# A hybrid attention and FFN kernel: the FFN's inner grid values turned in bf16 with their scales spread apart by DMA, and attention B's features normalized ahead

## The chip, the cores and the metric

The kernel runs on one core of a Trainium2 chip. The metric is the device time of one execution in microseconds (us). A core has five engines that run side by side, each with its own queue in order: TensorE (PE in the profile, with its weight loads as PEld), VectorE (DVE), ScalarE (ACT), GpSimd (POOL) and SyncE (SP), which here only issues DMAs.

## The reference

The input x is 4 x 2048 tokens of width 256, all in float32. Four residual layers follow each other; each adds to x a function of the layer-normalized x:

- attention A: three projections, a random-feature map of the whole-tensor-normalized q and k, and `out = s * v / s`, so that the output is the value projection times a ratio near one.
- FFN, used twice with the same weights. Its linear layers work on values quantized in blocks of 16 and turned back: `q = GRID[searchsorted(MID, |x/scale|)] * sign(x) * scale`, with `scale = max|x| / 6` of the block. The gate and up projections go to 704 columns, `h = silu(gate) * up` is quantized in its turn (44 blocks of 16 in a row), and the down projection brings it back to 256.
- attention B, between the two FFNs: q, k, v and two gates are projected; q and k are normalized in each head of 16; the four rows of the batch are mixed for each token (`A = k v^T` summed over the batch, then `q A`), gated, and projected by Wo.

## The kernel before, in words

The 2048 positions are cut into 16 groups of 128. A group holds a tile x of 128 partitions by 4 batch rows by 256, and goes through attention A, FFN, attention B and FFN; a batch row of it in an FFN is called a tile here, so there are 16 x 2 x 4 = 128 FFN tiles. All matmuls take float32 operands.

A first pass loads all of x, sums its Gram matrix for the whole-tensor norm of attention A (L551), and folds and centers the weights: `center` (L903 on) takes the column means out of a weight matrix, so that a projection of x itself is a projection of x minus its mean.

The order of the work is not that of the code. Every operation is recorded with an engine, an assumed duration, a rank and the buffers that it reads and writes; `Plan.order` (from L114) plays these through with its assumed durations and writes out one order for each engine. Ranks are the group's entry in the table BEGIN plus an offset, with a little noise from a seed. Operations marked `port=True` are kept from running on DVE and POOL at the same time. Buffers come from small pools, and an operation is only placed where a buffer of its pool is free. The chip then runs each engine's list strictly in order, with semaphores between the engines; a list does not adapt when a duration was assumed wrongly.

An FFN tile (`ffn_tile`) goes like this:

1. PE: two halves of 352 columns, each with a gate bank and an up bank, 4 recorded matmul calls for a half (L1363).
2. ACT: silu of the gate bank (L1384). DVE: times the up bank into h (L1395).
3. `quantize`: DVE takes the block maxima and their reciprocals (L384, L385); ACT divides the maxima by 6 (L1192); DVE scales h (L389); ACT makes magnitudes in bf16 (L395); DVE rounds to the grid by adding and subtracting a large number (L402, L405); POOL multiplies by the scales (L1220), 704 columns in float32.
4. PE turns the six blocks of 128 columns (L1418, matmuls against an identity; the last two blocks overlap, since 704 is not a multiple of 128), into two banks of 4 and 2 blocks; ACT copies each to SBUF as hqT (L1430).
5. PE: six matmul calls of 256 columns against wdT (L1441). DVE adds the result to x (L339 in the first FFN, L1473 in the second, after which SP stores the row, L1481).

`ffn_in` normalizes x (ACT, L378), quantizes it in the same manner on 128 x 1024 tiles, POOL included, and turns it (L1122, L1129).

`attention_b` turns x as it is (L1122, PE, and L1129, ACT), projects it (L1145) to a bank of 512 columns (q and k) and one of 288 (v and gates), and DVE drains each bank with one operation, `bank * rstd + bias` (L1528). `root` makes rstd of the variances on POOL in 8 small steps, 6 for attention B, which needs no offset.

The profile counts each float32 matmul call against weights twice (x2048 for 1024 calls in L1363) and each float32 turn once.

Of the kernel before, what the change touches and what calls it, by code (L numbers as in the profile page):

```python
# [18 lines left out]
P = 128  # L19
# [230 lines left out]
def kernel(  # L250
# [56 lines left out]
    def load_x(dst, j):  # L307
# [10 lines left out]
    bqkB = one([P, 2 * D], "bqkB")  # L318
    bvgB = one([P, NV], "bvgB")
# [4 lines left out]
    norm_tiles = {k: one([P, NJ, 6, S], f"norms_{k}") for k in ("a", "f1", "b", "f2")}  # L324


    moments = one([P, NJ, S, 6], "moments")
    both = one([P, NJ, S, 2], "both")
    norms = {
        (k, j): [t[:, j, n, :] for n in range(6)]  # L330
# [26 lines left out]
    def take_rstd(key, step):  # L357
# [5 lines left out]
        elif step == 2:  # L363
            nc.gpsimd.tensor_mul(t, y, y)
        elif step == 3:
            nc.gpsimd.tensor_mul(t, t, v)
        elif step == 4:
            nc.gpsimd.tensor_scalar(t, t, -0.5, 1.5, ALU.mult, ALU.add)
        elif step == 5:
            nc.gpsimd.tensor_mul(y, y, t)  # L370
        elif step == 6:
            nc.gpsimd.tensor_mul(off, sums, y)
        else:
            nc.gpsimd.tensor_scalar(off, off, -1.0 / D, 0.0, ALU.mult, ALU.add)
# [29 lines left out]
    def from_sum(a, m):  # L404
        nc.vector.scalar_tensor_tensor(a, m, FLOOR, a, ALU.max, ALU.subtract)  # L405
# [18 lines left out]
    tiles("sx", 3, [P, 3, S * D // BLK], fp)  # L424
    tiles("sil", 2, [P, HF], fp)
    tiles("qa", 4, [P, FF], fp)
    tiles("qm", 2, [P, FF], fp, BF16)
    tiles("sh", 5, [P, 3, FB], fp)
    tiles("hqT", 2, [P, 6, P], fp)
    tiles("tok", 1, [P, S, D], fp)  # L430
    tiles("vz", 2, [P, S, 2 * D], bp)
# [12 lines left out]
    def first_pass():  # L444
# [5 lines left out]
        for b in XN:  # L450
            nc.gpsimd.memset(b.ap[:, :, D : D + 1], 1.0)
        WQK, PROD, WNAT = (plan.given("pp", 0) for _ in range(3))
# [4 lines left out]
        wnat = WNAT.ap.rearrange("p (t c) d -> p t c d", t=2)  # L457
        MK, GROW, MAPT, G = (plan.given(p, 0) for p in ("vz", "tok", "sc", "fac"))
# [32 lines left out]
        for at, token, fn in (  # L491
# [23 lines left out]
            (34.1, ("bB", 0), over_rows(bqkB[:, :D], b_bq)),  # L515
            (34.2, ("bB", 0), over_rows(bqkB[:, D:], b_bk)),
            (34.3, ("bB", 0), over_rows(bvgB[:, :D], b_bv)),
            (34.4, ("bB", 0), over_rows(bvgB[:, D : D + NH], b_br)),
            (34.5, ("bB", 0), over_rows(bvgB[:, D + NH :], b_bw)),
# [105 lines left out]
        for ns in together:  # L625
            for n in ns:
# [21 lines left out]
                for s in range(S):  # L648
# [8 lines left out]
                        [("moments", j, s)],  # L657
# [5 lines left out]
            seen = [("moments", i, s) for i in js for s in range(S)]  # L663
# [239 lines left out]
        def center(at, w, n, tokens):  # L903
# [10 lines left out]
            def dve():  # L914
                for c in range(KC):
                    nc.vector.scalar_tensor_tensor(
                        w[:, c, :], mm.ap[:, :n], -1.0 / D, w[:, c, :], ALU.mult, ALU.add
# [3 lines left out]
            op("DVE", 0.2 + n / 450.0, at + 2, dve, [(mm, 0)], tokens)  # L921
# [16 lines left out]
        center(AHEAD + 50.0, wqkB, 2 * D, [("wqkB", 0)])  # L938
        center(AHEAD + 54.0, wvgB, NV, [("wvgB", 0)])
# [139 lines left out]
        (-91, -18, -64, 57, -73, -13),  # L1079
        (35, 82, 59, 126, 299, 228),  # L1080
        (293, 397, 356, 450, 375, 486),
        (370, 404, 412, 488, 580, 596),
        (433, 471, 475, 573, 630, 638),
        (485, 530, 525, 621, 687, 715),
        (518, 567, 530, 673, 716, 745),
        (588, 644, 630, 743, 560, 676),
        (602, 669, 606, 752, 637, 771),
        (671, 699, 702, 801, 719, 886),
        (714, 797, 826, 891, 958, 1069),
        (788, 865, 877, 996, 972, 1083),  # L1090
        (839, 971, 923, 1030, 822, 1063),
        (879, 1027, 930, 1059, 1017, 1130),
        (910, 1041, 830, 1087, 873, 1230),
        (953, 1023, 1012, 1151, 918, 976),
    ]

    def group(j):
# [65 lines left out]
        def root(at, key):  # L1163

            n = 6 if key[0] == "b" else 8
# [11 lines left out]
        def quantize(at, src, parts, a, m, q, us):  # L1177

            v = blocks_of(src)
            op(  # L1180
# [6 lines left out]
            )  # L1187
            op(
                "ACT",
                0.25,  # L1190
                at + 2,
                lambda: nc.scalar.mul(q.ap[:, 1, :], q.ap[:, 0, :], 1.0 / 6.0),  # L1192
                [(q, 0)],
                [(q, 1)],
# [10 lines left out]
            op("ACT", us["abs"], at + 2, lambda: to_steps(m.ap, a.ap), [(a, 0)], [(m, 0)])  # L1205
            for i, step in enumerate((to_sum, from_sum)):
                op(
                    "DVE",
                    us["pass"],
                    at + 4 + 0.1 * i,  # L1210
                    lambda step=step: step(a.ap, m.ap),
                    [(m, 0)],
                    [(a, 0)],
                    port=True,
                )
            op(
                "POOL",
                us["scale"],
                at + 6,
# [6 lines left out]
            )  # L1226

# [96 lines left out]
        def ffn_in(at, k):  # L1324
# [4 lines left out]
            for s in range(S):  # L1329
# [10 lines left out]
            quantize(  # L1340
# [6 lines left out]
                {"amax": 1.8, "pass": 1.19, "abs": 1.0, "scale": 1.93},  # L1347
            )
            return turn(
# [4 lines left out]
        def ffn_tile(at, k, s, xqT):  # L1354
            h, qa, qm, sh = (plan.buf(p) for p in ("h", "qa", "qm", "sh"))
            for half in range(2):
# [46 lines left out]
            quantize(  # L1403
# [6 lines left out]
                {"amax": 1.32, "pass": 0.86, "abs": 0.74, "scale": 1.4},  # L1410
            )
            hqT = plan.buf("hqT")
            for i0, i1 in ((0, 4), (4, 6)):
# [360 lines left out]
```

## Time and profile before

| | us |
|---|---|
| median of 3 runs | 1522.6 (1521.85 to 1522.8) |
| the profiled execution | 1523.6 |
| its span, first to last instruction | 1521.6 |
| PE busy | 1499.4 (99%) |
| PE weight loads busy | 1073.0 (71%) |
| DVE busy | 1387.3 (91%) |
| ACT busy | 810.1 (53%) |
| POOL busy | 693.2 (46%) |

The mean granted TensorE clock is 0.997 of full speed. In a row of groups, "x2048 | 637.7, 459 | 0.3" reads: 2048 instructions, together busy for 637.7 us, 459 ns from start to end of one on average, and 0.3 us of idle time before them. Matmuls overlap each other, so the mean of one times their number is more than their busy time; the spacing of a matmul's starts, which is what the next one has to wait, is read from a timeline. In a timeline, a line gives start, length, engine, line of the code, operation and the number of equal instructions merged into it.

### The profile page before, as it was taken

What the parts mean: (1) busy time and instruction counts of PE and PEld (TensorE: products, weight loads), DVE (VectorE), ACT (ScalarE), POOL (GpSimd) and SP (SyncE); (2) the same over time, 40 slices, a digit from 0 to 9 for tenths busy, and PEclk for the clock granted to TensorE, in tenths of its full rate; (3) what the DMA queues carried; (4) which work ended last, traced back from release to release, by engine and by line L of the source; (5) the groups of instructions that cost most, each with busy time, mean ns of one, the idle gap of its engine ahead of it and who ended that gap; (6) DMA issues with size and microseconds to landing.
All of it is one profiled execution on the core that took longest, in us unless ns stands there. A gap on an engine that the chain in (4) does not pass through costs nothing.

```text
span 1521.6 us, 18780 instructions
## 1 busy us (share of the span) xinstructions
PE 1499.4 (99%) x6362; PEld 1073.0 (71%) x6362; DVE 1387.3 (91%) x2266; ACT 810.1 (53%) x1745; POOL 693.2 (46%) x750
## 2 busy tenths in 40 slices
PE   7989999999999999999999999999999999999999
PEld 6847676766767666677667676776677677667777
DVE  6899999899899998989999999898989899999985
ACT  6666455555636556455554455465654455445443
POOL 5444454444536254444543543544453644553531
PEclk9999999999999999999999999999999999999999
DMA  8300000000000000000000000100000000000000
GB/s 268 100 1 1 1 1 0 29 0 11 18 4 7 18 4 5 8 4 22 4 18 8 8 21 14 42 5 4 5 7 1 0 1 1 5 11 14 14 22 21
DMA packets 29025, 27.68 MB, mean 18 GB/s; under 512 B 3585, under 2 KB 28673, under 8 KB 28929
## 3 DMA queue, kind: packets, MB, share of 16 engines
q1 hardware_dynamic: 28928, 26.49, 5.6%
q8 instruction: 50, 0.82, 0.2%
q14 instruction: 47, 0.38, 0.1%
HBM read 18.09 MB, written 8.39 MB: 17 GB/s over the span
## 4 chain that ended last, share of the span: by engine, by line
PE 80%; DVE 15%; issue 2%; ACT 1%; DMA 1%; POOL 0%; SPq 0%; DVEq 0%; POOLq 0%; ACTq 0%
PE bank L1363 32%; PE bank L1441 19%; PE bank L1145 18%; PE bank L1418 5%; PE bank L1122 3%; PE bank L551 2%; DVE h L1395 1%; DVE sh L384 1%; DVE pp L1546 1%; DVE qa L402 1%; DVE sc L1553 1%; DVE qa L389 1%; DVE qa L405 1%; DVE fac L1586 1%; DVE qk L1528 1%
## 5 line engine op out<-in xcount | busy, mean ns | idle before, releaser
L1363 PE MATMUL bank<-wguT,turned 128*128 128x352 f32 x2048 | 637.7, 459 | 0.3 <-DVE h L1395 0.3
L1363 PEld LDWEIGHTS bank<-wguT,turned 128*128 128x128 f32 x2048 | 379.7, 190 | 193.8 <-issue 11.7
L1220 POOL TENSOR_TENSOR qa<-qa,sh 128x704 f32<-128x704 f32 x128 | 203.0, 1586 | 407.6 <-DVE qa L405 315.6
L1441 PE MATMUL bank<-wdT,hqT 128*128 128x256 f32 x1536 | 350.6, 380 | 0.4 <-DVE x L1473 0.4
L1441 PEld LDWEIGHTS bank<-wdT,hqT 128*128 128x128 f32 x1536 | 289.5, 190 | 55.6 <-issue 4.5
L1430 ACT COPY hqT<-bank 128x512 f32<-128x512 f32 (+1 forms) x256 | 114.5, 479 | 94.6 <-PE bank L1418 92.4
L1384 ACT ACTIVATE sil<-bank 128x352 f32<-128x352 f32 x256 | 116.1, 458 | 88.9 <-PE bank L1363 83.5
L395 ACT ACTIVATE qm<-qa 128x704 bf16<-128x704 f32 (+1 forms) x136 | 105.9, 781 | 106.4 <-DVE qa L389 103.4
L1395 DVE TENSOR_TENSOR h<-sil,bank 128x352 f32<-128x352 f32 x256 | 128.8, 508 | 19.1 <-PE bank L1363 11.3
L1654 POOL TENSOR_TENSOR pp<-vg,sc 128x1024 f32<-128x1024 f32 x64 | 131.0, 2066 | 31.8 <-DVE tok L1675 27.1
L402 DVE SCALAR_TENSOR_TENSOR qa<-qm,qa 128x704 f32<-128x704 bf16 (+1 forms) x136 | 125.5, 924 | 12.0 <-ACT qm L395 11.9
L389 DVE SCALAR_TENSOR_TENSOR qa<-sh,h 128x704 f32<-128x704 f32 x128 | 126.7, 994 | 2.2
L1145 PE MATMUL bank<-wvz,turned 128*128 128x512 f32 x256 | 119.4, 604 | 5.5 <-ACT turned L1129 4.0
L405 DVE SCALAR_TENSOR_TENSOR qa<-qm,qa 128x704 f32<-128x704 bf16 (+1 forms) x136 | 122.1, 898 | 3.0
L384 DVE TENSOR_REDUCE sh<-h 128x44 f32<-128x748 f32 x128 | 119.1, 931 | 3.7
L1145 PE MATMUL bank<-wqkB,turned 128*128 128x512 f32 x256 | 119.6, 593 | 0.0
L1129 ACT COPY turned<-bank 128x512 f32<-128x512 f32 x160 | 86.8, 588 | 58.3 <-PE bank L1122 58.1
L1418 PEld LDWEIGHTS bank<-ident,qa 128*128 128x128 f32 x768 | 90.7, 141 | 29.0 <-issue 12.0
L1220 POOL TENSOR_TENSOR qax<-qax,sx 128x1024 f32<-128x1024 f32 x32 | 68.3, 2135 | 87.2 <-DVE qax L405 81.8
L1418 PE MATMUL bank<-ident,qa 128*128 128x128 f32 x768 | 105.0, 273 | 1.2 <-POOL qa L1220 1.1
L1192 ACT ACTIVATE sh<-sh 128x44 f32<-128x44 f32 x128 | 30.6, 239 | 119.2 <-DVE sh L384 116.3
L1145 PEld LDWEIGHTS bank<-wvz,turned 128*128 128x128 f32 x256 | 47.2, 193 | 54.3 <-issue 41.5
(180 smaller groups left out, 2150.1 us busy)
## 6 DMA issues: line engine op xcount, KB each, us to landing
x<-in_L_attn_a_x_dram SPq DMA_DIRECT2D x23, 512.0 KB, 5.5
out_dram<-x SPq DMA_DIRECT2D x64, 128.0 KB, 1.7
hqT<-in_L_ffn_w_down_dram SPq DMA_DIRECT2D x2, 352.0 KB, 3.9
hqT<-in_L_ffn_w_gate_dram SPq DMA_DIRECT2D x5, 128.0 KB, 3.9
hqT<-in_L_ffn_w_up_dram SPq DMA_DIRECT2D x5, 128.0 KB, 2.7
x<-in_L_attn_a_x_dram SPq DMA_DIRECT2D x4, 128.0 KB, 2.3
pp<-in_L_attn_a_Wq_dram SPq DMA_DIRECT2D x2, 256.0 KB, 5.6
pp<-in_L_attn_a_Wk_dram SPq DMA_DIRECT2D x2, 256.0 KB, 5.2
```

Source lines behind the costliest of these rows:

```text
L384: nc.vector.tensor_reduce(amax, src, AX.X, ALU.max, apply_absolute_value=True)
L389: nc.vector.scalar_tensor_tensor(blocks(a), over_blocks(rs), -6.0 * BELOW, src, ALU.mult, ALU.mult)
L402: nc.vector.scalar_tensor_tensor(a, m, FLOOR, a, ALU.max, ALU.add)
L405: nc.vector.scalar_tensor_tensor(a, m, FLOOR, a, ALU.max, ALU.subtract)
L1145: nc.tensor.matmul(bank.ap[:, :n], lhs.ap[:, c, s * P : (s + 1) * P], w[:, c, :], start=(c == 0), stop=(c == KC - 1),)
L1220: lambda: nc.gpsimd.tensor_mul(blocks(a.ap), blocks(a.ap), over_blocks(q.ap[:, 1, :])),
L1363: nc.tensor.matmul(bank.ap[:, :HF], xqT.ap[:, c, s * P : (s + 1) * P], w[:, c, cols], start=(c == 0), stop=(c == KC - 1),)
L1384: lambda g=g, sil=sil: nc.scalar.activation(sil.ap, g.ap[:, :HF], AF.Silu),
L1395: lambda u=u, sil=sil, half=half: nc.vector.tensor_mul(h.ap[:, half * FB // 2 : (half + 1) * FB // 2, :BLK], blocks(sil.ap), blocks(u.ap[: ...
L1418: nc.tensor.transpose(bank.ap[:, (i - i0) * P : (i - i0 + 1) * P], qa.ap[:, HC[i] : HC[i] + P], ident,)
L1441: nc.tensor.matmul(o.ap[:, :D], hqT.ap[:, i, :], wdT[:, i, :], start=(i == 0), stop=(i == 5),)
L1654: nc.gpsimd.tensor_mul(pv.ap.rearrange("p t (n e) -> p t n e", e=HD), vg.ap[:, :, :D].rearrange("p t (n e) -> p t n e", e=HD), over_blocks ...
```

## The change

The FFN's inner quantization (step 3 and 4 above) is split. `quantize` becomes `to_grid`, which ends with the rounded grid values, without scales. These are small multiples of one half and are written as bf16 into qm. Now there are two paths for a tile:

- values: PE turns six blocks in bf16 (L1494 in the new file), all into one bank; ACT copies the 768 columns, as bf16, into qm (L1505).
- scales: PE turns the 44 block maxima (L1279, float32, 44 x 128 out), ACT divides them by 6 into sT (L1287), and SP issues six DMAs (L1296), each of which reads 8 rows of sT 16 times and writes a 128 x 128 part of hqT.

POOL multiplies hqT by the turned values in place (L1513, 768 columns, one operand float32 and one bf16), and the down matmuls (L1524) follow. The outer quantization in `ffn_in` keeps its POOL product (`times_scales`).

In attention B, ACT normalizes x into a new tile xh (rstd and offset, as in the FFN), xh is turned in place of x, and the two banks are drained by plain copies on ACT (L1619). The biases are folded into the weights: `center` subtracts (mean - bias/256) per row of the weights, and `root` takes 8 steps and ends with an offset raised by one for attention B, so that every feature carries an added 1 which brings in the bias.

Pools: sx 3 to 2, qa 4 to 3, qm 2 to 4 (768 columns), sh 5 to 4, hqT 2 to 3, and new sT (2) and xh (1). Statistics of the first pass and the biases move into tiles that are unused then; norm tiles are shared by two groups. The table BEGIN has new values throughout and the seed of the order goes from 2 to 10, so nearly all of the order of the work is new.

The core of the diff:

```diff
@@ to_grid (was quantize)
-        def quantize(at, src, parts, a, m, q, us):
+        def to_grid(at, src, parts, a, m, q, us, to=None):
...
-            op(
-                "ACT",
-                0.25,
-                at + 2,
-                lambda: nc.scalar.mul(q.ap[:, 1, :], q.ap[:, 0, :], 1.0 / 6.0),
-                [(q, 0)],
-                [(q, 1)],
-            )
...
+            op(
+                "DVE",
+                us["pass"],
+                at + 4.1,
+                lambda: from_sum(a.ap, m.ap[:, :n], to and to.ap[:, :n]),
+                [(a, 0), (m, 0)],
+                [(to or a, 0)],
+                port=True,
+            )
@@ new
+        def scales_turned(at, q, dst):
+            bank, sT = plan.buf("bank"), plan.buf("sT")
+            op("PE", 0.12, at,
+                lambda: nc.tensor.transpose(bank.ap[:FB, :P], q.ap[:, 0, :], ident),
+                [(q, 0)], [(bank, 0)])
+            op("ACT", 0.22, at + 0.5,
+                lambda: nc.scalar.mul(sT.ap, bank.ap[:FB, :P], 1.0 / 6.0),
+                [(bank, 0)], [(sT, 0)])
+            def spread():
+                n = P // BLK
+                for i, f in enumerate(HC):
+                    src = sT.ap[f // BLK : f // BLK + n]
+                    nc.sync.dma_start(
+                        dst.ap[:, i, :], src.unsqueeze(1).to_broadcast([n, BLK, P])
+                    )
+            op("SP", 4.9, at + 1, spread, [(sT, 0)], [(dst, "scale")], land=3.3)
@@ ffn_tile
             hqT = plan.buf("hqT")
-            for i0, i1 in ((0, 4), (4, 6)):
...
+            scales_turned(at + 8, sh, hqT)
+            bank = plan.buf("bank")
+            def turn_hidden():
+                for i, f in enumerate(HC):
+                    nc.tensor.transpose(
+                        bank.ap.bitcast(BF16)[:, i * P : (i + 1) * P],
+                        qm.ap[:, f : f + P],
+                        ident16,
+                    )
+            op("PE", 0.36, at + 14, turn_hidden, [(qm, 0)], [(bank, 0)])
+            op("ACT", 0.73, at + 15,
+                lambda: nc.scalar.copy(qm.ap, bank.ap.bitcast(BF16)[:, : 6 * P]),
+                [(bank, 0)], [(qm, 0)])
+            op("POOL", 1.6, at + 16,
+                lambda: nc.gpsimd.tensor_mul(
+                    hqT.ap, hqT.ap, qm.ap.rearrange("p (c n) -> p c n", n=P)
+                ),
+                [(qm, 0), (hqT, "scale")], [(hqT, 0)], port=True)
@@ attention_b
-            xT = turn(at, X, range(S), lambda: X.ap)
+            xh = plan.buf("xh")
+            for s in range(S):
+                op("ACT", 0.52, at + 1.0 + 0.1 * s,
+                    lambda s=s: normalize(xh.ap[:, s, :], xs(s), key, s),
+                    [(X, s), (key, "rstd")], [(xh, s)])
+            xT = turn(at + 1.5, xh, range(S), lambda: xh.ap)
...
-                        "DVE",
+                        "ACT",
                         ds,
                         at + 5 + 3 * s,
-                        lambda bank=bank, n=n, bvec=bvec, dst=dst, s=s, rstd=rstd: (
...
+                        lambda bank=bank, n=n, dst=dst, s=s: nc.scalar.copy(
+                            dst.ap[:, s, :], bank.ap[:, :n]
                         ),
@@ center
+                if bias:
+                    less, part = bias[0], 1.0 / D
+                    nc.vector.scalar_tensor_tensor(
+                        less, mm.ap[:, :n], -1.0, less, ALU.mult, ALU.add
+                    )
@@ end
-    order = plan.order(2)
+    order = plan.order(10)
```

## The prediction

> **What bounds the kernel now.** First the page's busy times, the chain of work that ended last, and PE's own waits (engine, line, whom it waited for: us in total, times, longest).
>
> ```profile
> PE 1499.4 (99%) x6362; PEld 1073.0 (71%) x6362; DVE 1387.3 (91%) x2266; ACT 810.1 (53%) x1745; POOL 693.2 (46%) x750
> ```
> ```profile
> PE 80%; DVE 15%; issue 2%; ACT 1%; DMA 1%; POOL 0%; SPq 0%; DVEq 0%; POOLq 0%; ACTq 0%
> ```
> ```profile
> PE bank L551 <- ACT vg L378: 10.0, 1, 10.0
> PE bank L1145 <- ACT turned L1129: 4.0, 1, 4.0
> PE bank L1418 <- POOL qa L1220: 1.1, 2, 0.6
> ```
>
> PE never waits long after its start. A busy PE can still be a slack one, so I take issue spacings from a timeline with full queues:
>
> ```profile
> 904.26 2.53 PE L1363 MATMUL bank<-wguT,turned 128*128 128x352 f32 x8
> ...
> 906.63 0.82 PE L1418 MATMUL bank<-ident,qa 128*128 128x128 f32 x6
> ...
> 907.28 5.35 PE L1441 MATMUL bank<-wdT,hqT 128*128 128x256 f32 x24
> ...
> 912.47 4.90 PE L1363 MATMUL bank<-wguT,turned 128*128 128x352 f32 x16
> ```
>
> Starts: 2.37 us for 8, so 296 ns at 352 columns; 0.65 for 6, so 108 ns for a turn; 5.19 for 24, so 216 ns at 256. All are 0.84 ns a column. Times the counts: L1363 606, L1441 332, L1145 337 (512 at 512 columns, 256 at 288, 256 at 256), 1408 turns 152, the first pass about 54: together **1481 us of issue in a span of 1521.6**. The other 41 are 10.0 at the start, 4.0 once, some 3 after the last matmul, and 24 in small gaps. PE is the bound; DVE at 91% is next.
>
> **The change, part by part.** The rows that it touches, the first four from the groups kept apart by shape:
>
> ```profile
> L1430 ACT COPY hqT<-bank 128x512 f32<-128x512 f32 x128 | 74.5, 585 | 51.6 <-PE bank L1418 49.8
> L1430 ACT COPY hqT<-bank 128x256 f32<-128x256 f32 x128 | 47.7, 373 | 43.0 <-PE bank L1418 42.6
> L1528 DVE SCALAR_TENSOR_TENSOR qk<-bank,norms_b,bqkB 128x512 f32<-128x512 f32 x64 | 46.8, 737 | 13.9 <-PE bank L1145 13.6
> L1528 DVE SCALAR_TENSOR_TENSOR vg<-bank,norms_b,bvgB 128x288 f32<-128x288 f32 x64 | 32.1, 503 | 3.6 <-PE bank L1145 1.8 <-POOL norms_f L372 1.0 <-POOL norms_b L370 0.2
> ```
> ```profile
> L1220 POOL TENSOR_TENSOR qa<-qa,sh 128x704 f32<-128x704 f32 x128 | 203.0, 1586 | 407.6 <-DVE qa L405 315.6
> L1418 PE MATMUL bank<-ident,qa 128*128 128x128 f32 x768 | 105.0, 273 | 1.2 <-POOL qa L1220 1.1
> ```
>
> *PE, on the path.* 768 float32 turns become bf16, and 128 float32 turns of scales (128 columns, 108 ns: 13.8 us) are new. No bf16 matmul is in the trace. A turn of float32 weights and data costs 108 ns; bounds for bf16 are no gain (108) and half for half the bytes (54). I take 54: turns and products of float32 cost the same 0.84 ns a column, so the price goes with what is streamed, and bf16 streams half of it (an inference, not a row). -768 x 0.054 + 13.8 = **-27.6 us**; at 108 it is +13.8.
>
> The Trainium skill, "TensorE: Matmul & The Clock Gate", section "Back-to-back issue gap", speaks against it: a steady stream of weight loads and 128-column matmuls runs at about 81 ns each. By that estimate the turns save 20.7 and the part is worth -6.9, which the losses below eat up: no change. No row here has such a pair in bf16.
>
> *DVE, beside PE.* 128 drains leave (46.8 + 32.1 = 78.9 us); the first pass gains two small operations. 1387 - 79 = 1308 over some 1500, 87%. L405 now writes bf16; its row stays at 0.91. Nothing is late next here: between any two FFN tiles of the new order DVE's work falls ever further behind PE's.
>
> *ACT, beside PE.* Out: L1430, 122.2 us. In: 128 copies of 768 columns at (585-373)/256 = 0.83 ns a column, so 797 ns, 102 us; 64 drains at 0.585 and 64 at 0.40, 63; 64 normalizations at 0.593, 38. The scaling of 128 tiny tiles stays at 0.24. 810 + 81 = 891, 60%.
>
> *POOL, beside PE.* 768 columns for 704 (undisturbed 1.39 us): 1.52, or 1586 x 768/704 = 1730 with waits, +18 us; 32 more root steps of 0.32, +10. 48%. If a bf16 operand were slower I bound it by another 0.5, 64 us of an engine that is half idle.
>
> *Normalizing ahead.* Attention B's turn now waits for eight POOL steps (909.48 to 913.90 in the timeline, 4.4 us) and four normalizations (2.4 us). Other groups' FFN tiles lie beside it; without them it would be 16 x 6.8 us.
>
> *SP and the spread.* 768 new DMAs. Issue time from SP's timeline, landing time and packets from the page:
>
> ```profile
> 35.10 0.54 SPq L479 DMA_DIRECT2D pp<-in_L_attn_a_Wk_dram  x1
> 35.69 0.48 SPq L479 DMA_DIRECT2D wqkB<-in_L_attn_b_Wk_w_dram  x1
> ```
> ```profile
> q1 hardware_dynamic: 28928, 26.49, 5.6%
> hqT<-in_L_ffn_w_up_dram SPq DMA_DIRECT2D x5, 128.0 KB, 2.7
> ```
>
> Six issues take 3.0 us, the last lands 2.7 later: 5.7; SP is busy for 384 us. Queued behind are 64 stores and 8 loads of x, needed late. 5.6% of 16 x 1521.6 us over 28928 packets is 47 ns a packet; 768 packets a tile over 16 engines are 2.3 us. No row has SBUF as the source: I bound the spread by 2.7 (one landing alone) and 11 us (twice the estimate), and take 5.7, whose issue part is measured.
>
> The skill, "DMA: Bandwidth & Descriptors", section "Why a DMA increments its semaphore by 16 and not by 1", says that the slowest dimensions, here 8 rows and 128, set the engines: 8 of 16. By that estimate a DMA moves for 0.75 us, longer than an issue, the spread takes some 7 us and is still hidden.
>
> *New waits, read from the built order of the changed kernel* with PE's spacings summed between two of its instructions:
> - From the end of a down product to the next one on the same hqT (SP waits for it, then POOL): at least 10.6 us of PE work, save three at the very end with 5.2, 6.3 and 6.3. Needed: 5.7 + 1.52 + semaphores, about 8. Hidden but for the tail.
> - From a tile's last hidden matmul to the turn of its scales, which holds up all of PE's list: 11 tiles under 3.0 us. Needed: 0.46 + 0.51 + 0.93 + 0.43 and semaphores, about 3. At 3.0 the shortfalls sum to 3 us, at 3.5 to 9; I take 5.
> - From the value turns to the down product: 10 tiles under 3.0, needed 0.80 + 1.52 + semaphores; shortfalls 2 to 4, I take 1, as the rest shares stalls with the former.
>
> *The tail.* Before:
>
> ```profile
> 1508.14 0.89 DVE L405 SCALAR_TENSOR_TENSOR qa<-qm,qa 128x704 f32<-128x704 bf16 x1
> ...
> 1509.20 1.39 POOL L1220 TENSOR_TENSOR qa<-qa,sh 128x704 f32<-128x704 f32 x1 [6.22 <-PE bank L1441]
> ...
> 1513.05 5.45 PE L1441 MATMUL bank<-wdT,hqT 128*128 128x256 f32 x24
> ```
>
> PE works until 1518.5. In the new order the last tile's hqT is freed only by the down product four places from the end, which itself stands behind the last turns: spread, POOL and product follow one another (5.7 + 1.5 + 2.6) where three others of 2.6 cover 5.2. **+4 us.**
>
> **The sum.** 1521.6 - 27.6 + 5 + 1 + 4 = 1504 of span. Part of the 24 us of gaps should go with DVE's relief, for which I take 2 off: 1502. The profiled execution took 1523.6, 2.0 more than its span, and the median of the runs, 1522.6, is 1.0 below that; so the same 1.0 goes on top of the span: **1503**.
>
> **Rivals.**
> - *DVE was half the bound.* The chain gives it 15%. If ten more of the 24 us go: 1490. For it: DVE at 97% from 1200 to 1400. Against: PE's listed waits on DVE are under 2 us.
> - *The turns gain little* (65 to 85 ns): 1511 to 1527. For it: weight loads appear in their own instructions in the new order. Against: loads in the turns of before (141 ns each) hide entirely.
> - *It doesn't do what it says:* a bf16 turn costs 108 ns, 1503 + 41.5 = 1544, slower.
> - *The spread becomes PE's wait.* One mechanism: SP may refill an hqT only after its down product, and PE's next one on it waits for the landing and POOL. Shortfalls in the order: 16 us in all if the way takes 11, 23 at 12, 44 at 14. The tail's 4 stand for the 6 that the order has at 8. The gain of some 20 is gone where the sum is 26, near 12.3, that is, at a spread of 10 instead of 5.7; at 14 the time is about 1503 + 44 - 6 = 1541. For it: no SBUF source, no repeated row in the trace. Against: SP's issues, and 10.6 us of cover.
>
> **Chances.** Forecast .56 (own range 1495 to 1511); DVE's relief .10; little gain .14 (.09 faster, .05 within); 108 ns .08; the spread .12. A measurement of this kernel tells 0.2% from no change. Faster .75, within 0.2% .05, slower .20. The range reaches from 1487 (relief) to 1528 (turns at 85, or a spread of 10 with the forecast's turns); the two slow cases past it are the .20 left out. The unknown prices run on to 1544.
>
> **What would show it.** Turns: starts of the bf16 matmuls 54 ns apart, the six done in 0.33 us. Path: PE still at 98% or more, its issue sum 1453. Spread: hqT landing within 6 us of the first issue, POOL's product waiting for ACT's copy and not for a DMA. Scales: PE's waits on L385 in single microseconds. DVE near 87%. Wrong if PE's idle time grows by over 20 us, or if turns cost over 80 ns.

## The result and the profile after

The changed kernel takes 1546.35 us (median of 6 runs, 1544.01 to 1549.92), the kernel before 1521.78 (1521.25 to 1522.8): a ratio of 1.0163 (1.0150 to 1.0177). It is slower by 25 us, where 20 us less were predicted. The profiled execution has a span of 1542.0 us and a time of 1544.01.

From the page of the changed kernel, the busy times and the chain of work that ended last:

```profile
PE 1488.9 (97%) x6490; PEld 1045.9 (68%) x6490; DVE 1390.9 (90%) x2140; ACT 880.4 (57%) x1808; POOL 749.7 (49%) x782
...
PE 70%; DVE 16%; issue 4%; POOL 4%; ACT 3%; DMA 2%; SPq 0%; POOLq 0%; ACTq 0%; DVEq 0%
```

PE has less work in a longer span. DVE lost 126 instructions, 78.9 us of them drains, and is busier than before (1387.3). PE's own waits (engine, line, whom it waited for: us in total, times, longest) were 10.0, 4.0 and then single us before; now a row of others stands behind the first:

```profile
PE bank L567 <- ACT vg L378: 8.9, 1, 8.9
PE bank L1524 <- POOL hqT L1513: 8.0, 8, 2.5
PE bank L567 <- ACT qk L378: 7.4, 3, 4.0
PE bank L1494 <- DVE qm L405: 5.6, 4, 2.1
```

The wanted part of the change is there. A timeline of the changed kernel (start, length, engine, line):

```profile
906.33 0.50 PE L1494 MATMUL bank<-ident,qm 128*128 128x128 bf16 x6
...
906.66 0.71 PE L1147 MATMUL bank<-ident,xh 128*128 128x128 f32 x5
```

Six bf16 turns start within 0.33 us, 55 ns each.

**A ledger of PE.** Busy time counts pipelined matmuls too long, so I part PE's time otherwise: for each matmul, the spacing of its start from the start before, less the median spacing of that earlier matmul's line (a line with several weight tiles is kept apart by them). The medians sum to the work, the rest is waiting. The columns count time from the first matmul's start, some 9 us into the span. From the traces, us:

| kernel | work | waiting | of it in 0 to 200 | 200 to 1400 | 1400 on |
|---|---|---|---|---|---|
| before | 1499.0 | 9.1 | -0.5 | 9.3 | 0.3 |
| after | 1472.6 | 57.0 | 15.3 | 26.4 | 15.4 |

In every kernel the first pass's Gram matmuls of 257 and of 129 columns share one median, so some 13 us of waiting in the first 200 us are counted as work. Kept apart by shape, the work is 1485.8 us before and 1459.2 after, near the 1481 and 1453 of the prediction, and the waiting 22.4 and 70.4. The differences are the same either way, and they count. The work fell by **26.4 us** (predicted: 27.6). The waiting grew by **48**, and in three places: at the start, throughout, and in the last 140 us. The experiments go by these three.

### The profile page after: what moved, and what is told of

It reads as the page before. It is cut to its first block, busy times and chain, and to the rows that moved or that the text cites. A ratio compares the mean times of both kernels' runs of the same rounds, so it can differ in the third digit from the quotient of the medians.

```text
span 1542.0 us, 21280 instructions
## 1 busy us (share of the span) xinstructions
PE 1488.9 (97%) x6490; PEld 1045.9 (68%) x6490; DVE 1390.9 (90%) x2140; ACT 880.4 (57%) x1808; POOL 749.7 (49%) x782
## 4 chain that ended last, share of the span: by engine, by line
PE 70%; DVE 16%; issue 4%; POOL 4%; ACT 3%; DMA 2%; SPq 0%; POOLq 0%; ACTq 0%; DVEq 0%
PE bank L1438 31%; PE bank L1524 16%; PE bank L1170 15%; PE bank L1147 3%; PE bank L1494 2%; DMA hqT<-sT 2%; DVE qa L402 2%; DVE qa L389 1%; DVE pp L1631 1%; DVE sh L384 1%; POOL hqT L1513 1%; DVE h L1470 1%; PE bank L567 1%; DVE qm L405 1%; DVE sc L1638 1%
## 5 line engine op out<-in xcount | busy, mean ns | idle before, releaser
L1513 POOL TENSOR_TENSOR hqT<-hqT,qm 128x768 f32<-128x768 f32 x128 | 232.0, 1818 | 367.7 <-ACT qm L1505 203.2
L1524 PE MATMUL bank<-wdT,hqT 128*128 128x256 f32 x1536 | 353.1, 382 | 9.7 <-POOL hqT L1513 8.0
L1524 PEld LDWEIGHTS bank<-wdT,hqT 128*128 128x128 f32 x1536 | 290.2, 191 | 70.0 <-POOL hqT L1513 17.8
L402 DVE SCALAR_TENSOR_TENSOR qa<-qm,qa 128x704 f32<-128x704 bf16 (+2 forms) x136 | 141.2, 1038 | 13.8 <-ACT qm L395 13.6
L1739 POOL TENSOR_TENSOR pp<-vg,sc 128x1024 f32<-128x1024 f32 x64 | 132.9, 2093 | 22.4 <-DVE tok L1760 19.3
L389 DVE SCALAR_TENSOR_TENSOR qa<-sh,h 128x704 f32<-128x704 f32 x128 | 139.4, 1098 | 0.8
L1505 ACT COPY qm<-bank 128x768 bf16<-128x768 bf16 x128 | 101.0, 795 | 60.3 <-PE bank L1494 58.5
L405 DVE SCALAR_TENSOR_TENSOR qm<-qm,qa 128x704 bf16<-128x704 bf16 x128 | 126.8, 993 | 4.6 <-POOL norms_f L363 0.5
L1263 POOL TENSOR_TENSOR qax<-qax,sx 128x1024 f32<-128x1024 f32 x32 | 74.0, 2314 | 102.0 <-DVE qax L405 69.9
L384 DVE TENSOR_REDUCE sh<-h 128x44 f32<-128x748 f32 x128 | 119.2, 931 | 4.1
L1631 DVE TENSOR_TENSOR pp<-qk 128x1024 f32<-128x1024 f32 x64 | 83.9, 1310 | 7.8 <-ACT qk L1619 7.6
L378 ACT ACTIVATE xn<-x,norms_f 128x256 f32<-128x256 f32 x128 | 67.8, 594 | 19.4 <-POOL norms_f L372 16.2
L1638 DVE TENSOR_REDUCE sc<-pp 128x64 f32<-128x1024 f32 x64 | 77.6, 1212 | 1.4
```

The source lines that it names most:

```text
L384: nc.vector.tensor_reduce(amax, src, AX.X, ALU.max, apply_absolute_value=True)
L389: nc.vector.scalar_tensor_tensor(blocks(a), over_blocks(rs), -6.0 * BELOW, src, ALU.mult, ALU.mult)
L405: nc.vector.scalar_tensor_tensor(a if to is None else to, m, FLOOR, a, ALU.max, ALU.subtract)
L1513: lambda: nc.gpsimd.tensor_mul(hqT.ap, hqT.ap, qm.ap.rearrange("p (c n) -> p c n", n=P)),
L1524: nc.tensor.matmul(o.ap[:, :D], hqT.ap[:, i, :], wdT[:, i, :], start=(i == 0), stop=(i == 5),)
L1739: nc.gpsimd.tensor_mul(pv.ap.rearrange("p t (n e) -> p t n e", e=HD), vg.ap[:, :, :D].rearrange("p t (n e) -> p t n e", e=HD), over_blocks ...
```

## The experiments

All times are medians; "before" was run beside each and stayed at 1521.6 to 1521.9. Where a kernel's order is called unchanged, only what an operation issues was edited, so that the lists of all engines stand as in the changed kernel.

### First four: spread, product, VectorE, seed

**e1, no spread.**

```diff
             def spread():
                 n = P // BLK
+                return
...
-                    hqT.ap, hqT.ap, qm.ap.rearrange("p (c n) -> p c n", n=P)
+                    hqT.ap, ones.unsqueeze(1).to_broadcast([P, 6, P]),
+                    qm.ap.rearrange("p (c n) -> p c n", n=P),
```

> The order of the changed kernel, unchanged, but the 768 DMAs that spread the scales are left out and POOL's product multiplies by ones (scales left out of the down product). Theory A, the spread is what comes late (27 of POOL's products wait for a landing, 120 us of POOL's idle time): without it the time is 1503 to 1512. Theory B, the port: POOL's product, no longer released by VectorE's rounding, runs beside VectorE's port operations and both get longer (VectorE 1391 us busy where 1308 was forecast): VectorE stays above 1370 and the time stays at 1535 to 1546. Theory C, the order itself is a worse one on the chip: 1535 to 1546 too.

Measured: 1537.7 us, DVE 1385.6. The spread costs 8.6 us and is not the main cause; theory A as put falls.

**e2, thin product.**

```diff
-                    hqT.ap, hqT.ap, qm.ap.rearrange("p (c n) -> p c n", n=P)
+                    hqT.ap[:, 0, :], hqT.ap[:, 0, :], qm.ap[:, :P]
```

> The order of the changed kernel, unchanged, with its DMAs, but POOL multiplies only 128 of the 768 columns (the other five blocks keep the scales alone as hqT), about 0.3 us instead of 1.64. Theory A (the spread is late): POOL still waits for the landings; only the product's own 1.3 us goes from the way, so 1525 to 1540. Theory B (the port): VectorE's rounding operations go back to 0.88 to 0.92 us each, VectorE falls to 1310 to 1330 us, and the time to 1500 to 1512. Theory C (the order): 1535 or more.

Measured: 1519.8 us, DVE 1322.7. DVE goes where theory B put it, the time does not quite, though it is nearest to B; and the edit also shortens each tile's way (from its turns to its down product) by 1.3 us; e5 and e18 part the two.

**e3, attention B's drains back on VectorE.**

```diff
-                        lambda bank=bank, n=n, dst=dst, s=s: nc.scalar.copy(
+                        lambda bank=bank, n=n, dst=dst, s=s: nc.vector.tensor_copy(
                             dst.ap[:, s, :], bank.ap[:, :n]
```

> The order of the changed kernel, but attention B's 128 drains are plain copies on VectorE again instead of ScalarE: 79 us more for VectorE (1391 to 1470), 63 less for ScalarE. Nothing of the computation changes. Theory A (the spread is late, VectorE has slack): within 10 us of the changed kernel, 1540 to 1556. Theory B (VectorE, lengthened at the port, is what PE waits for in small pieces): half of it or more shows, 1575 to 1625. Theory C says nothing of it.

Measured: 1585.2 us, with DVE 47 us busier (1437.6); the copies themselves take 71 us, other rows of DVE got shorter. So 47 us more of DVE's time cost 39: in this order DVE has little slack.

**e4, another seed.**

```diff
-    order = plan.order(10)
+    order = plan.order(7)
```

> The changed kernel with the seed of its order 7 instead of 10; same work, another order, which the planner's own assumed durations put 6 us behind. Theories A and B: the same losses, 1540 to 1560, VectorE again above 1370. Theory C (this one order happens to be bad on the chip): a time that is off by 15 us or more, in either direction, and not in the planner's proportion.

Measured: 1549.0 us, DVE 1377.7. Another seed of the same table of ranks loses as much, so it isn't this seed's luck.

### The port: what POOL does to VectorE

Three rows from the groups kept apart by shape (busy, mean ns, idle before), first of the kernel before, then of the changed one:

```profile
L389 DVE SCALAR_TENSOR_TENSOR qa<-sh,h 128x704 f32<-128x704 f32 x128 | 126.7, 994 | 2.2
L402 DVE SCALAR_TENSOR_TENSOR qa<-qm,qa 128x704 f32<-128x704 bf16 x130 | 121.7, 937 | 12.0 <-ACT qm L395 11.9
L405 DVE SCALAR_TENSOR_TENSOR qa<-qm,qa 128x704 f32<-128x704 bf16 x130 | 118.4, 911 | 2.9
```
```profile
L389 DVE SCALAR_TENSOR_TENSOR qa<-sh,h 128x704 f32<-128x704 f32 x128 | 139.4, 1098 | 0.8
L402 DVE SCALAR_TENSOR_TENSOR qa<-qm,qa 128x704 f32<-128x704 bf16 x130 | 137.3, 1056 | 12.2 <-ACT qm L395 12.0
L405 DVE SCALAR_TENSOR_TENSOR qm<-qm,qa 128x704 bf16<-128x704 bf16 x128 | 126.8, 993 | 4.6 <-POOL norms_f L363 0.5
```

Same shapes, and each 80 to 120 ns longer. In the changed kernel's trace an L389 with no POOL operation beside it takes 885 ns (71 times), one that overlaps a POOL operation 1362 ns (57 times); L402 878 and 1264, L405 886 and 1165 (overlaps over 30 ns). That L405 now writes bf16 costs it nothing: alone it takes 886 ns in the kernel before too. A timeline shows how:

```profile
902.08 2.57 POOL L1739 TENSOR_TENSOR pp<-vg,sc 128x1024 f32<-128x1024 f32 x1
...
903.22 2.19 DVE L405 SCALAR_TENSOR_TENSOR qm<-qm,qa 128x704 bf16<-128x704 bf16 x1
```

POOL ends at 904.65; the pass that started at 903.22 ends 0.76 us after that, as if it had stood still until then. The Trainium skill, "SBUF — State Buffer", section "SBUF: two separate sides", says that DVE and GpSimd share a pair of ports as an exclusive lock, held for a whole instruction by whoever starts first, and that a DVE operation with two SBUF inputs contends for it with a GpSimd operation that reads SBUF; these rows agree. DVE's L384, which reads one SBUF tile, takes 931 ns in both kernels, alone or beside POOL.

The order keeps such operations apart by assumed durations; no product meets a DVE port operation in it. From starts and ends in the traces, POOL's 128 products overlap DVE's operations on two SBUF tiles (L389, L402, L405 and attention B's products and sums) for 50 us before (65 of the products) and 96 us after (89).

**e5, the product's load put beside the way.**

```diff
+                nc.gpsimd.tensor_mul(hqT.ap[:, 0, :], hqT.ap[:, 0, :], qm.ap[:, :P])
+                nc.gpsimd.tensor_mul(
+                    qm.ap[:, P:].rearrange("p (c n) -> p c n", n=P),
+                    hqT.ap[:, 1:, :],
+                    qm.ap[:, P:].rearrange("p (c n) -> p c n", n=P),
+                )
```

> As the thin product (POOL multiplies 128 of 768 columns into hqT, the down product waits for that alone; the other five blocks of hqT keep the scales alone), but right behind it POOL multiplies the other 640 columns into a tile that nobody reads before it is overwritten, so that POOL's load is about that of the changed kernel again while the way to the down product stays short. Theory B (the time is lost at the port that POOL and VectorE share): VectorE goes back to 1375 to 1395 us and the time to 1540 to 1552. Rival B2 (the thin product gained because the way scale, product, down product got 1.3 us shorter): the time stays at 1518 to 1526.

Measured: 1531.8 us, DVE 1373.2, between the two. Of e2's 26.5 us, 12.0 come back with POOL's load; the other 14.6 go with the way, or with the waits for landings that a short product absorbs. Not settled by this run.

**e6, products held back until VectorE has reached them.**

```diff
+                nc.gpsimd.tensor_copy(seen[:, n : n + 1], told[:, n : n + 1])
                 nc.gpsimd.tensor_mul(
...
+            for _ in tell.get(i, ()):
+                nc.vector.memset(told[:, n : n + 1], 0.0)
```

> The order of the changed kernel, with one rule more: each product on POOL also waits until VectorE has finished the port operation that the order puts before it (a one-column write on VectorE and a one-column copy on POOL carry the wait; 128 times some 0.06 and 0.2 us). Nothing of the computation changes. Theory B1 (the product runs ahead of VectorE because nothing of VectorE releases it any more, as in the kernel before): its starts ahead of VectorE go, the overlap of products and port operations falls from 105 us to 60 to 80, VectorE to 1350 to 1375, the time to 1530 to 1540. If it is POOL that is late and not early, or only the sum of the work at the port counts, nothing is gained: 1543 to 1555.

Measured: 1547.5 us, DVE 1373.8. The overlap fell from 96 to 56 us and DVE by 17, about as B1 asked, and the time didn't: PE's waits for hqT, 8.0 us in the changed kernel, are now

```profile
PE bank L1532 <- POOL hqT L1515: 12.7, 14, 2.9
```

What holds back a product also makes it late. B1 falls for the time.

**e7, the kernel before, with its product released through ScalarE.**

```diff
             def product():
+                if us["scale"] == 1.4:
+                    nc.scalar.copy(a.ap[:, :1], a.ap[:, :1])
                 nc.gpsimd.tensor_mul(
```

> The kernel before, its order unchanged, but the release of POOL's product goes through ScalarE: a one-column copy on ScalarE stands between VectorE's last rounding pass and the product (128 times some 0.2 us, and ScalarE's queue ahead of it). Theory B1 (a product that VectorE itself releases starts in the place that the order gave it, any other release sends it into VectorE's next port operations): VectorE's L389, L402 and L405 get longer by 30 to 80 ns each, VectorE 1400 to 1425 us, the time 1528 to 1545. Rival (only the amount of POOL's work counts): VectorE stays at 1385 to 1392, the time at 1521 to 1528, the way's 0.4 us being covered.

Measured: 1528.9 us (ratio 1.0048, 1.0031 to 1.0065), DVE 1398.9 (1387.3 before). The time is at the lower edge of B1's range and DVE just under it, but L389, L402 and L405 got only 1 to 24 ns longer where B1 asked 30 to 80, and the products overlap DVE's operations no more than before (46 us). So B1's mechanism isn't shown here. The kernel before, too, had no room for some 0.4 us more on each tile's way or for ScalarE's queue ahead of it, though PE hardly waited in it.

### The start: a shared tile

**e8, attention B's half alone** (normalized ahead, drains on ACT, biases in the weights, moments in qk; FFN of before).

```diff
+            xT = turn(at + 1.5, xh, range(S), lambda: xh.ap)
...
-                        "DVE",
+                        "ACT",
...
-    order = plan.order(2)
+    order = plan.order(106)
```

> Only the attention B half of the change (normalized ahead, drains as copies on ScalarE, biases in the weights), with the FFN of before; the changed kernel's table of ranks and the seed that the planner's own model likes best of 120 (1530.7; the kernel before is at 1526.7 by that model). VectorE loses 79 us of PSUM drains. Prediction's view (PE is the bound, relief of VectorE worth some us): 1510 to 1524. If the order's luck counts for as much as the work: 1524 to 1540.

Measured: 1541.0 us, though DVE fell to 1355.4. In the ledger its first 200 us lose some 15 us, as in the changed kernel. The timelines of the start show where. Changed kernel, the first pass (the bracket is the idle time before and what ended it):

```profile
23.67 2.07 ACT L378 ACTIVATE qk<-x,norms_a 128x256 f32<-128x256 f32 x4 [3.43 <-POOL norms_a L628]
24.91 5.28 PE L567 MATMUL bank<-qk 128*128 128x257 f32 x16 [3.96 <-ACT qk L378]
25.83 0.21 POOL L618 TENSOR_TENSOR norms_a<-qk 128x8 f32<-128x8 f32 x1 [1.91 <-ACT qk L378]
...
30.05 0.23 POOL L620 TENSOR_TENSOR qk<-qk 128x16 f32<-128x16 f32 x1 [3.73 <-PE bank L567]
```

The change put the first pass's moments into free columns of the tile qk, whose first 257 columns hold normalized x (and a one) for one in four of the groups' Gram products. ACT's write of x now waits for POOL's steps on the moments, POOL's steps wait for ACT's write and for PE's products, and PE waits for ACT: a ring of waits through one tile, on columns that have nothing to do with each other.

**e9, moments in a tile of their own.**

```diff
-        MOMENTS = XN[3]
+        MOMENTS = plan.given("xh", 0)
...
-            for at, n in ((D + 8, 6), (D + 8 + NJ * 6, 2))
+            for at, n in ((0, 6), (NJ * 6, 2))
```

> The changed kernel, its order unchanged, with one edit undone: the moments of the first pass no longer lie in columns of the tile qk, into which ScalarE also writes normalized x for the Gram matmuls, but in a tile of their own (xh, unused then). Theory E (sharing that tile makes ScalarE's normalization wait for POOL's steps on the moments and POOL's steps wait for PE's Gram matmuls, though the columns are disjoint): PE's waits on the line L567 go from 12 us to those of the kernel before, the first 200 us of the span lose some 12 us less, and the time is 1531 to 1537. Rival (the start is late because its loads land later, or by the new table of ranks): 1543 to 1549.

Measured: 1535.3 us (ratio 1.0087, 1.0073 to 1.0101), 11.0 less. Its timeline of the same place:

```profile
21.17 2.08 ACT L378 ACTIVATE qk<-x,norms_a 128x256 f32<-128x256 f32 x4
...
22.41 3.13 PE L567 MATMUL bank<-qk 128*128 128x257 f32 x16 [0.42 <-POOL norms_a L627]
```

**e10, that one part alone put into the kernel before.**

```diff
+        moments, both = (
+            XN[3].ap[:, :, at : at + NJ * n].rearrange("p s (j k) -> p j s k", k=n)
+            for at, n in ((D + 8, 6), (D + 8 + NJ * 6, 2))
+        )
```

> The kernel before, its order unchanged, with that one part of the change alone: the moments of the first pass in columns of the tile qk. Theory E: ScalarE's writes into qk and POOL's steps on the moments wait for each other in the first 60 us, PE's idle time there grows, the time is 1528 to 1537. Rival (the start has another cause): 1521 to 1524.

Measured: 1536.9 us (1.0099, 1.0085 to 1.0113), 15.0 more than before. One of PE's waits, in the kernel before and then in e10:

```profile
PE bank L551 <- ACT qk L378: 0.4, 1, 0.4
```
```profile
PE bank L553 <- ACT qk L376: 10.4, 3, 4.8
```

Theory E holds from both sides.

**e11, attention B's half with the moments apart** (on top of e8).

```diff
-        MOMENTS = XN[3]
+        MOMENTS = plan.given("xh", 0)
...
```

> Attention B's half of the change alone, as before, with the moments in a tile of their own. Theory E: 1527 to 1533 (1541 with the shared tile). The rest against the kernel before is then the order. Rival: 1538 to 1544.

Measured: 1529.8 us, 11.1 less than e8. The half with the drains off VectorE still gives no gain; its ranks are those of the changed kernel, so this says nothing final on the half itself.

### The end: the spread

First issue to last landing of a spread, from SP's issues and the packets of the queue in the changed kernel's trace: 7.16 us at least, median 7.5, at most 9.4. Six issues take 4.7 of it in the median:

```profile
L1296 SPq DMA_DIRECT2D hqT<-sT x768: 604/720/1792, 136.1 to 1529.9; - x192
```

(shortest, median and longest issue in ns). POOL waits for landings before 27 of its products (120 us of idle time of a half idle engine). At the very end there is nothing beside it. Changed kernel:

```profile
1520.15 10.61 SPq L1296 DMA_DIRECT2D hqT<-sT  x12
...
1528.93 1.64 POOL L1513 TENSOR_TENSOR hqT<-hqT,qm 128x768 f32<-128x768 f32 x1 [5.35 <-DMA hqT<-sT]
...
1534.33 1.64 POOL L1513 TENSOR_TENSOR hqT<-hqT,qm 128x768 f32<-128x768 f32 x1 [3.76 <-DMA hqT<-sT]
1536.02 2.46 PEld L1524 LDWEIGHTS bank<-wdT,hqT 128*128 128x128 f32 x12 [2.94 <-POOL hqT L1513]
```

Two spreads can only begin when a down product has freed an hqT; spread, product and down product follow one another.

**e12, moments apart and no spread.**

```diff
-        MOMENTS = XN[3]
+        MOMENTS = plan.given("xh", 0)
...
             def spread():
                 n = P // BLK
+                return
...
```

> The changed kernel, its order unchanged, with the moments in a tile of their own and without the DMAs of the spread (POOL's product multiplies by ones, the scales are left out). If both losses add: 1546 less 12 for the start less 9 for the spread, 1522 to 1528. What is then left against a sum of issue that is 26 us smaller than before is the port and the longer way of a tile: POOL's product and VectorE's lengthened operations. If the losses cover each other: 1528 to 1537.

Measured: 1526.7 us. The two losses add (11.0 and 8.6). In the ledger e9 and e12 differ by 8.6 after 1400 us and by 1.8 between 200 and 1400 (a wait of some 2 us lies at the border; counted from the span's start it is 6.7 and 3.5): in the steady part the spread is all but hidden.

**e15, the last group's hqT in idle tiles** (on top of e9).

```diff
-            hqT = plan.buf("hqT")
+            late = k == 2 and j in (14,)
+            hqT = plan.buf("pp" if late else "hqT")
...
```

> As the changed kernel with the moments in a tile of their own, table and seed unchanged, with the one more edit that the four tiles of group 14's second FFN take their hqT from three idle tiles pp, so that the last spreads need not wait for the down products that free hqT. If the tail's three waits for landings (5.4 and 3.8 us of POOL's in the last 16 us) go: 1527 to 1532 against 1535. If another wait takes their place: 1533 to 1537.

Measured: 1529.3 us, 6.1 less than e9: most of the tail's loss goes, with the computation whole.

### What is left: the product at the port

**e13, another order** (e15 with new ranks and seed).

```diff
     BEGIN = [
-        (-174, -176, -141, -364, -123, -178),
+        (9, -524, -189, -332, -72, -190),
...
-    order = plan.order(10)
+    order = plan.order(145)
```

> The changed kernel's whole work, with the moments in a tile of their own, hqT of the four tiles of group 14's second FFN in three tiles pp that are idle by then, and a new table of ranks and seed. They were chosen by playing each written order through with every engine strictly in order and the port of VectorE and POOL given to whoever comes first: by that, waits at the port fall from 354 to 285 us in sum (270 for the kernel before) and the end by 35 us. Theory F (the remaining loss is the order's: it was written for port operations that never meet): VectorE falls to 1350 to 1375 us and the time to 1500 to 1512, faster than the kernel before. Rival (the loss is the work's own, of a nearly full VectorE and the longer way): 1526 to 1535, as with the moments apart alone.

Measured: 1536.6 us, 7 more than e15, though DVE fell by 30 to 1360.3. Theory F falls as put: in this order the products overlap DVE's operations less (73 us, 94 in e15), and PE waits more in the middle (37 us of the ledger between 200 and 1400, 27 in e15).

**e14, the kernel before in an order chosen likewise** (the table alone; its first row and the others).

```diff
-        (-91, -18, -64, 57, -73, -13),
+        (-105, 156, -51, 66, 51, -11),
...
```

> The kernel before, its work unchanged, in an order chosen in the same manner (a third of the search's length): by that playing through, 5 us are to be had. PE loses only some 9 us to waits there, so theory F gives 1515 to 1521; the rival (orders make no difference beyond the port) 1520 to 1526.

Measured: 1519.2 us, ratio 0.9985 (0.9976 to 0.9994): 2.5 us less than before, the fastest of the kernels that compute everything. It lies in theory F's range and just under the rival's.

**e16, e13 without its spread.**

```diff
             def spread():
                 n = P // BLK
+                return
...
```

> The searched order of the changed work (e13), without the DMAs of the spread; POOL's product multiplies by ones (the scales are left out). If that order lost to late landings what it won at the port: 1506 to 1516, 20 us or more under e13's 1537, and below the order of the changed kernel without spread (1527). If the landings cost it no more than they cost the order of the changed kernel outside its tail (2 to 3 us): 1530 to 1535.

Measured: 1529.5 us, 7.1 less than e13, just under the second range. The landings cost this order 7.1 us, where they cost e15's 2.6 (e15 to e12, in which the tail's tiles are as they were): some 4.5 of the 7.3 us by which e13 is slower than e15. Without a spread it is still 2.8 us slower than e12, with 15 us less of DVE's time (1371.5). What it loses there stays open.

**e17 and e18, in the changed kernel's order: product off the way and off the port, then back on the port.** e17 is e12 with a thin product, the first line below; e18 has all three.

```diff
+                nc.gpsimd.tensor_mul(hqT.ap[:, 0, :], ones, qm.ap[:, :P])
+                rest = qm.ap[:, P:].rearrange("p (c n) -> p c n", n=P)
+                nc.gpsimd.tensor_mul(rest, ones.unsqueeze(1).to_broadcast([P, 5, P]), rest)
```

> The changed kernel, its order unchanged, moments apart, no spread, and POOL's product only 128 of 768 columns times ones (scales left out, five blocks of hqT constant). If spread and product are separate losses they add: 1527 less 20 to 26, so 1501 to 1507, which with 1473 us of PE issue leaves about the waits that the kernel before had. If they are one loss seen twice: 1515 to 1522.

> As e17, but POOL multiplies the other 640 columns too, right behind, into a tile that nobody reads before it is overwritten: POOL's load at the port is back, the way to the down product stays short. The port's share is the difference to e17, the way's share the difference to e12 (1527): by the two runs with spread (e2 and e5) 12 of the port and 8 to 14 of the way, so 1513 to 1519. If all of it is the port: 1524 to 1528. If all is the way: 1501 to 1507.

Measured: e17 1505.0 us (0.9889, 0.9874 to 0.9904), e18 1520.8 (0.9993, 0.9984 to 1.0002). The busy times of e17, then of e18:

```profile
PE 1477.8 (98%) x6490; PEld 1042.7 (69%) x6490; DVE 1323.5 (88%) x2140; ACT 881.4 (59%) x1808; POOL 567.6 (38%) x785
```
```profile
PE 1480.6 (98%) x6490; PEld 1040.6 (69%) x6490; DVE 1379.5 (91%) x2140; ACT 879.8 (58%) x1808; POOL 780.1 (51%) x913
```

DVE's instructions are the same in both, and 212 us of POOL's work whose result nobody reads make them 56 us longer, and the kernel 15.8. The product on the way costs 5.9 (e12 to e18), so e18 lies just above its range: more of the port and less of the way than expected. The chain that ended last, e17 first, goes through DVE for three times the share:

```profile
PE 87%; DVE 8%; ACT 2%; issue 1%; POOL 1%; DMA 0%; SPq 0%; DVEq 0%; ACTq 0%; POOLq 0%
```
```profile
PE 63%; DVE 24%; ACT 5%; issue 5%; POOL 3%; DMA 0%; SPq 0%; ACTq 0%; DVEq 0%; POOLq 0%
```

A busier POOL also does its own other work later: ACT's normalizations (L378, xn and xh) wait for its steps on the norms 27 us in e18 and 14 in e17. So the 15.8 is the port in the main, and how much of it is POOL's queue was not parted. One row of DVE in each, e17 first:

```profile
L389 DVE SCALAR_TENSOR_TENSOR qa<-sh,h 128x704 f32<-128x704 f32 x128 | 124.0, 977 | 0.8
```
```profile
L389 DVE SCALAR_TENSOR_TENSOR qa<-sh,h 128x704 f32<-128x704 f32 x128 | 134.6, 1060 | 0.8
```

The ledger, with the parts taken away one after the other, us:

| kernel | time | work | waiting | 0 to 200 | 200 to 1400 | 1400 on |
|---|---|---|---|---|---|---|
| after | 1546.4 | 1472.6 | 57.0 | 15.3 | 26.4 | 15.4 |
| e9, moments apart | 1535.3 | 1472.5 | 49.3 | 3.8 | 28.5 | 17.1 |
| e12, and no spread | 1526.7 | 1472.5 | 39.3 | 4.1 | 26.7 | 8.5 |
| e18, and a short way | 1520.8 | 1472.5 | 32.8 | 2.2 | 26.6 | 4.1 |
| e17, and off the port | 1505.0 | 1472.6 | 18.4 | 2.0 | 13.9 | 2.6 |

Each part has its place: the shared tile the start, spread and way mostly the end, the port the middle.

## Why the prediction was wrong, point by point

The forecast was 1503, the range 1487 to 1528. Taken away one after the other, four parts are worth 11.0, 8.6, 5.9 and 15.8 us, 41.4 in all, and leave 1505.0 us. The first two came with the change. The last two are what POOL's product costs in this order. The kernel before has such a product too (203 us of POOL); it was not taken out there, but PE waits for only 9.3 us between 200 and 1400 us in it, where the changed kernel waits for 26.4. That e17 ends near 1503 does not bear the forecast out: it leaves out the spread and five sixths of the product, which the forecast held to be hidden.

- *The turns.* Right, though inferred without a row: 55 ns for 54, the work 26.4 us less for 27.6. The 81 ns of the Trainium skill ("TensorE: Matmul & The Clock Gate", section "Back-to-back issue gap") for a stream of such pairs, which the prediction weighed against itself, do not hold here; the measurement decides. The rival of 108 ns is out.
- *DVE.* The step that failed: "1387 - 79 = 1308 over some 1500, 87%. ... Nothing is late next here". The 79 us did leave, and 82 came back, 62 of them in seven rows of unchanged shapes (L389 in both shapes, L402, L405 and three of attention B's products and sums): the durations had been taken as fixed. The rows of DVE had POOL's interference in them already (L389 994 ns on average, 883 alone), and how much interference there is was left to change with the order. With DVE at 90% again its time counts: e3 gives 0.8 us for each us of DVE's growth, e17 and e18 0.3 (15.8 for 56). The prediction counted POOL's product as "POOL, beside PE" and found its engine half idle; what it takes from DVE was never priced.
- *The moved statistics.* No term at all, not even at nothing: 11.0 us (15.0 when put into the kernel before). The prediction asked of each *engine* what stands behind it, never of this tile who else writes it. Keeping the moments in a tile of their own (e9) takes nothing from what the change gains.
- *The spread.* Hidden, as predicted, up to the tail; "5.7" should have been 7.5, within its bounds, because an issue takes 0.72 us and not 0.5; the prediction's second estimate, some 7, was nearer. The tail was put at 4 and is most of 8.6. Its sum doesn't give the 4 either: 5.7 + 1.5 + 2.6 less 5.2 is 4.6, and three products of 2.6 us are 7.8, not 5.2.
- *The value turns to the down product.* Put at 1 us, with "the rest shares stalls": the product's length on that way is worth 5.9 (e12 to e18), 4.4 of it after 1400 us.
- *Rival "the spread becomes PE's wait".* Its mechanism ran, at 8.6 us, where 26 were said to turn the sign. Its time came out nearly right for another reason. *Rival "DVE's relief"*: there was no relief.
- *What would show it.* "Wrong if PE's idle time grows by over 20 us" was the right alarm: the waiting grew by 48. Three signs failed with it: DVE is at 90% and not near 87, no spread lands within 6 us, and POOL waits for a DMA before 27 products.

Not settled: why POOL's products meet DVE's operations twice as long as before (96 us for 50). That DVE no longer releases them is at most a part of it (e6: 17 us of DVE's time, without a gain; e7: 12, but not by longer overlaps). Nor why an order with 30 us less of DVE's time (e13) is no faster, beyond the 4.5 us of landings, and so whether any order would let the changed work win. The smaller pools (sx, qa, sh) and a spread by another queue were not tried.

## What to carry to other kernels

Work taken off an engine gives back less than its rows say when the rest of its work gets longer; where two engines share a port, a mean duration from the profile holds the present collisions, so price it once alone and once beside the other engine, and ask what moves. When a tile gets a second use, list every reader and writer of both uses: here waits were made by tile, and a ring through three engines can come of columns that never meet. An edit "to make room" deserves a term in the sum like any other.

## What the runs showed of the hardware

- DVE operations on two SBUF inputs stretch beside POOL's: in the changed kernel 878 to 886 ns alone, 1165 to 1362 beside (L389, L402, L405); L384, with one SBUF input, stays at 931.
- A bf16 turn of 128 columns takes 55 ns in a row although each weight load takes 98 (PEld of L1494 51.5 us busy for 768).
- An issue of a DMA from SBUF to SBUF with a source read 16 times takes SP 0.72 us in the median (0.60 to 1.79), and its last packet lands 2.8 us after the last of six issues (median).
- A wait of PE cost more than itself at the start: after 3.96 us of idling, sixteen Gram matmuls took 5.28 us, where they took 3.13 in e9. The spacing of most at 257 columns was 426 to 431 ns, for 216 to 219 in most of e9's; the granted clock from 24.9 to 29.9 us is 0.51, in e9 from 22.4 to 25.4 us 1.00.
